# Bounded gathers with cleared row tiles in layer 2, adjacency pieces between x loads, and table 1 stored from GpSimd

## Chip, core and metric

The kernel runs on one core of one Trainium2 chip. The metric is the device time of one execution in microseconds (us). Lines such as L804 are lines of the kernel before. The engines are TensorE (PE in the profile), VectorE (DVE), ScalarE (ACT), GpSimd (POOL) and SyncE (SP).

## What is computed

Two graph attention layers on a graph of N = 2048 nodes, for a batch of 8, with 64 features, and a residual with two layer norms:

```python
mask = adj + eye(N) > 0
def _gat_layer(h, mask, b):            # h: [..., N, D]
    scores = einsum('...nd,...md->...nm', h, h)
    attn = softmax(where(mask, scores, NEG), axis=-1)
    return einsum('...nm,...md->...nd', attn, h) + b
h    = einsum('bnc,hdc->bhnd', x, Wh)              # 4 heads
z    = leaky_relu(concat_heads(_gat_layer(h, mask, bh)), 0.2)
h2   = einsum('bnk,dk->bnd', z, Wo)
z2   = leaky_relu(_gat_layer(h2, mask, bo), 0.2)
out  = layernorm(x + layernorm(z2) * gamma + beta)
```

The adjacency is sparse: the chance of a link is 0.0039 on the mean and falls with the square roots of both node numbers, so the first nodes have far more neighbours than the others.

## The kernel before

**Tiling.** The first 32 nodes (the hub) are computed against all nodes. The other 2016 are cut into 168 *sets* of 12 nodes. For each set the kernel finds the at most 128 nodes that any of its members is linked to, as a list of 128 node numbers, and gathers their rows. A row holds one node for all 8 batches: 4 pairs of 1 + 64 + 64 + 1 numbers (the ones give the softmax sums), 520 float32, 2080 bytes. Table 1 holds x, table 2 holds h2. Where a set has fewer than 128 neighbours, the places left over are *unlinked*: their index is N or more, and a mask takes them out of the sums later.

**Hub phase** (0 to 131 us). Loop L966 runs over 16 blocks of 128 nodes. In each step: load_x (L462) clears the ends of a row tile on VectorE and issues two DMAs of x from ScalarE; save_x (L469) stores the row tile, 260 KB, into table 1, from ScalarE; hub_scores (L597) multiplies, subtracts a mask on VectorE (L605) and takes the exp on ScalarE (L607); turn_x (L592) transposes the next block; hub_values (L611) sums. Meanwhile 34 *pieces* of the adjacency are loaded and prepared by load_adj (L674): the DMAs from SyncE, 440 KB a piece, into one of three raw tiles, then a conversion (L687) and diagonal marks (L695, L698) on GpSimd. more(n) (L943) takes the next n pieces. Before the loop stand more(6) (L949) and more(4) (L955), in it more(1) from i = 6 on (L969) and more(2) at i = 2 (L991). make_keys (L720) turns pieces into lists on TensorE, pick (L735) chooses the neighbours of 60 sets on VectorE.

**Layer 1** (131.7 to about 620 us). Loop L1133 runs over 84 groups of two sets: gather (L801, the instruction is L804) fetches the rows of table 1 on GpSimd, five groups ahead; then transposes, scores, mask (L839), exp, values and projections; the rows of table 2 are stored from SyncE (L910). Jobs for layer 2 are spread over it by ahead_of_second (L1125), one for each second group: among them memsets of shared tiles (L1126) and link() (L1066). In the last steps and after the loop (L1220) hub_step (L1118) computes the hub of layer 2 by parts: scores on TensorE (L1092), the mask's subtraction on VectorE (hub_lift2, L1101), exp on ScalarE (L1104), values.

**Layer 2** (627 to 904 us). There are 36 row tiles rowt2, and the 168 gathers use them in turn (rows2, L1235). The first 36 are issued ahead (L1242), the others nine steps ahead in loop L1425, which handles four sets per step u: turn2 (L1392) transposes the rows, scores2 (L1246) multiplies, exp, keep_scores (L1267) applies the mask *linked*, values2 (L1275) sums, and norm (L1289) does the layer norms, mostly on VectorE, in jobs spread over later steps.

**Bounds.** A gather may be given bounds_check = N - 1 with oob_is_err=False: places with a larger index are left out, and the tile keeps what it held. All gathers of layer 1 have it, and those of layer 2 from the 37th on. The first 36 of layer 2 haven't, as their tiles hold whatever lay in that memory; link() masks their indices to 0 to N - 1 instead, so that they fetch all 128 rows:

```python
bound = {} if layer == 2 and s < 36 else dict(bounds_check=N - 1, oob_is_err=False)
...
nc.vector.tensor_scalar(index2[:, :36], index2[:, :36], N - 1, None, OP.bitwise_and)
```

**What sets the order.** The schedule is manual: each engine runs its instructions in the order in which the program writes them, and engines wait for each other by semaphores, which the framework derives from the tiles read and written. DMAs are issued by the engine named (nc.sync, nc.scalar, nc.gpsimd), in the place where they stand in its program, and an issue waits like any other instruction.

Of the kernel before, what the change touches and what calls it, by code (L numbers as in the profile page):

```python
# [36 lines left out]
OP = mybir.AluOpType  # L37
# [322 lines left out]
def fast_kernel(ctx: ExitStack, tc: tile.TileContext, x, adj, Wh, bh, Wo, bo, gamma, beta, out, flag):  # L360


    nc = tc.nc
    B, N, C = x.shape
    H, D, _ = Wh.shape
    P = 128
# [61 lines left out]
    table1 = dram.tile([N, ROW], F32, name="table1")  # L428
# [9 lines left out]
    index = const.tile([P, NS], I32, name="index")  # L438
    index2 = const.tile([P, NS], I32, name="index2")
# [11 lines left out]
    xrow = {}  # L451
# [10 lines left out]
    def load_x(i):  # L462
        t = xrow[i] = rows_tile(f"x{i}")
        nc.vector.memset(t[:, :, 0:PW:PW - 1], 1.0)
        for p in range(2):
            nc.scalar.dma_start(out=t[:, :, 1 + p * D:1 + (p + 1) * D],
                                in_=x[p::2, i * P:(i + 1) * P, :].rearrange("q n c -> n q c"))

    def save_x(i):  # L469
        nc.scalar.dma_start(out=table1[i * P:(i + 1) * P, :], in_=xrow[i].rearrange("n q c -> n (q c)"))  # L470

    NCH = HALFN
    in_round = [min(FIRST, NS - FIRST * r) for r in range(NR)]
# [77 lines left out]
    def hub_mask():  # L551
        for k in range(2):
            nc.vector.tensor_scalar(hubm[:, k * NCH:(k + 1) * NCH], hubraw[k], 1.0, 0.0, OP.min, OP.max)
        nc.vector.tensor_tensor(hubm[:, :HUB], hubm[:, :HUB], identb[:HUB, :HUB], OP.max)
        pm = two("pm")
        for m in range(NB):
            nc.tensor.matmul(pm[:, m // 8, (m % 8) * HUB:(m % 8 + 1) * HUB], hubm[:, m * P:(m + 1) * P],
                             identb[:HUB, :HUB], start=True, stop=True)
        for k in range(2):
            nc.vector.tensor_scalar(  # L560
                maskh[:, k * 8:(k + 1) * 8, :].rearrange("p m (n h) -> p (m n) h", h=H),
                pm[:, k, :8 * HUB].unsqueeze(2).to_broadcast([P, 8 * HUB, H]), 0.0, 255.0, OP.is_equal, OP.mult)
        nc.vector.tensor_scalar(maskt[:HUB, NHB, :], pm[:HUB, 0, :HUB], 0.0, 255.0, OP.is_equal, OP.mult)
# [22 lines left out]
    def hub_columns():  # L586
        py = two("pyh")
        for h in range(H):
            nc.tensor.matmul(py[:, 0, h * P:(h + 1) * P], gram[:, h, :], xT[:, :, :HUB], start=True, stop=True)
        nc.vector.tensor_copy(yh.rearrange("p (m h) -> p m h", h=H), py[:, 0, :].rearrange("p (h m) -> p m h", h=H))  # L590

    def turn_x(i):  # L592
        tp = two(f"px{i}")
        turn(tp[:, 0, :], xrow[i])
        nc.scalar.copy(xT[:, :, i * P:(i + 1) * P], tp[:, 0, :].rearrange("c (q n) -> c q n", q=Q))

    def hub_scores(i):  # L597
        sp = two(f"sh{i}")
        for q in range(Q):
            for p in range(2):  # L600
                for r in range(2):
                    nc.tensor.matmul(sp[half(r), p, q * HW:(q + 1) * HW], xT[half(p), q, i * P + r * 64:i * P + (r + 1) * 64],
                                     yh[half(p), q * HW:(q + 1) * HW], start=True, stop=True)
        e = es[i % 2]
        nc.vector.tensor_tensor(e.rearrange("p (a q n) -> p a q n", a=2, q=Q), sp.rearrange("p a (q n) -> p a q n", q=Q),  # L605
                                maskh[:, i, :].unsqueeze(1).unsqueeze(1).to_broadcast([P, 2, Q, HW]), OP.subtract)
        nc.scalar.activation(e, e, AF.Exp, bias=shifts[:, 0:1], scale=1.0)  # L607
# [3 lines left out]
    def hub_values(i):  # L611

        for q in range(Q):
            for p in range(2):
                for u in range(2):
                    c0 = (p * Q + q) * HW + u * 64
                    o0 = q % 2 * PO + p * K1
                    nc.tensor.matmul(hubo[half(u), q // 2, o0:o0 + K1], es[i % 2][:, c0:c0 + 64], xrow[i][:, q, sums(p)],
                                     start=(i == 0 and q % 2 == 0 and p == 0), stop=(i == NB - 1), skip_group_check=True)
# [54 lines left out]
    def load_adj(r, t, m):  # L674

        s0 = FIRST * r + S10 * t
        ns = min(S10, NS - s0)
        np_ = ns * SET
        raw = early.tile([120, NCH], I32, tag="raw", name=f"raw{r}_{t}_{m}", bufs=3)
        for s, n0, n in flipped(s0, ns):  # L680
            nc.sync.dma_start(out=raw[s - s0:s - s0 + n], in_=adj[n0:n0 + n, m * NCH:(m + 1) * NCH])
        nc.sync.dma_start(out=raw[ns:np_], in_=byset[1:, s0:s0 + ns, m * NCH:(m + 1) * NCH])
        if m == 0:
            ahead[r, t] = early.tile([120, 2, HALFN + 80], BF16, tag="a", name=f"a{r}_{t}", bufs=5)
        a = ahead[r, t]
        w = NCH // 2
        nc.gpsimd.tensor_scalar(a[:np_, :, m * w:(m + 1) * w], raw[:np_].rearrange("p (c h) -> p h c", h=2),  # L687
                                1.0, 0.0, OP.min, OP.max)
        if m == 1:

            c1 = (REST + s0) // 2
            for h in range(2):
                for s, n0, n in flipped(s0, ns):
                    d = a[:np_, h, n0 // 2:(n0 + n) // 2]
                    nc.gpsimd.affine_select(out=d, in_=d, pattern=[[-2, n // 2]], base=s0 - s - h,  # L695
                                            channel_multiplier=1, compare_op=OP.not_equal, fill=1.0)
                d = a[:np_, h, c1:c1 + NS // 2 * (SET - 1)].rearrange("p (k c) -> p k c", k=SET - 1)[:, :, :ns // 2]
                nc.gpsimd.affine_select(out=d, in_=d, pattern=[[-ns, SET - 1], [-2, ns // 2]], base=-h - ns,  # L698
                                        channel_multiplier=1, compare_op=OP.not_equal, fill=1.0)
# [9 lines left out]
    def make_powers6():  # L709
        g = in_round[NR - 1] // S10 % 3  # L710
        d = powers6[:last * SET, g, 10 * g:10 * g + last]
        for k in range(SET):
            nc.gpsimd.affine_select(out=d, in_=d, pattern=[[-1, last]], base=-last * k, channel_multiplier=1,
                                    compare_op=OP.not_equal, fill=float(1 << k))
# [85 lines left out]

    def gather(table, s, layer, new):  # L801
        t = rows[layer, s] = new(f"g{layer}_{s}")
        bound = {} if layer == 2 and s < 36 else dict(bounds_check=N - 1, oob_is_err=False)
        nc.gpsimd.indirect_dma_start(out=t.rearrange("n q c -> n (q c)"), out_offset=None, in_=table,  # L804
                                     in_offset=bass.IndirectOffsetOnAxis(ap=(index if layer == 1 else index2)[:, s:s + 1], axis=0), **bound)

    def own_rows(m):

# [134 lines left out]
    def more(n):  # L943

        for _ in range(n):
            if pieces:
                load_adj(*pieces.pop(0))

    more(6)  # L949
    hub_mask()  # L950
    hub_mask_sets()
    weights()
    turn_x(0)
    hub_columns()
    more(4)  # L955
    picks = []

    def some(n):
        for _ in range(n):
            if picks:  # L960
                picks.pop(0)()
# [4 lines left out]
    for i in range(NB):  # L966
        if i + 4 < NB:
            load_x(i + 4)
        more(1 if i >= 6 else 0)  # L969
        save_x(i)  # L970
        if i == 3:
            nc.gpsimd.memset(rall[:, NG:, :], 1.0)
            nc.gpsimd.memset(rall2, 1.0)
            nc.gpsimd.memset(over, 0.0)
            for k in range(SET):
                nc.gpsimd.memset(bits[:, k:k + 1], N << k)
            nc.gpsimd.memset(shifts[:, 2:3], EPS)
            nc.gpsimd.memset(ones, 1.0)
            for t in rowts + xbs:
                nc.gpsimd.memset(t, 1.0)  # L980
            if last:
                make_powers6()
        hub_scores(i)
        if i + 1 < NB:
            turn_x(i + 1)
        if i:
            hub_values(i - 1)
        if i in (2, 6):
            make_keys(0, i // 6, two)
            if i == 2:  # L990
                more(2)  # L991
            if i == 6:
                picks = pick(0)
        some(4)
# [70 lines left out]
        nc.vector.tensor_tensor(index2, index2, node, OP.add)  # L1065

    def link():
        nc.vector.tensor_scalar(index2[:, :36], index2[:, :36], N - 1, None, OP.bitwise_and)
        nc.vector.tensor_scalar(linked, mask.rearrange("p s (k h) -> p s k h", h=H)[:, :, :, 0], 0.0, None, OP.is_equal)

    W2 = D + 2
# [161 lines left out]
    rowt2 = [late.tile([P, Q, PW], F32, name=f"rows2_{k}", bufs=1) for k in range(36)]  # L1233
# [7 lines left out]
        hub_block(8 + k, hrows[k])  # L1241
    for u in range(9):  # L1242
        for s in sets[u]:
            gather(table2, s, 2, rows2)

    def scores2(u):  # L1246
# [255 lines left out]
```

## Time and profile before

| what | us |
|---|---|
| median of 5 runs | 902.87 (901.93 to 907.39) |
| the profiled execution | 905.84 |
| its span, first to last instruction | 904.0 |
| busy: PE, DVE, ACT, POOL | 740.8, 602.8, 504.3, 516.2 |
| L804, gathers of layer 1 (168) | 178.5 busy, 1.062 each |
| L804, gathers of layer 2 (168) | 179.9 busy, 1.071 each |
| first and last gather of layer 2 start | 627.27, 856.60 |
| bytes of queue 0 (the gathers and other GpSimd DMAs) | 69.27 MB |

The span's mean granted TensorE clock is 0.942. The profile's timelines list, for each engine, start, length, line, operation, output and input tiles, and in square brackets the idle time ahead of the instruction and what ended it. "issue" means that nothing in the profile was waited for. The page's slices show TensorE busy over eight tenths from about 160 us on, with a dip in the slices at 610 to 650, where the profile shows both the lowest granted clock of the later part and the most DMA traffic (297 GB/s).

### The profile page before, as it was taken

The page shows a single profiled execution, that of the slowest core. Times are in us where ns is not written, and L with a number is a line of the kernel's source. Part 1 is how long each engine was busy: PE and PEld are TensorE (multiplying, and loading weights), DVE is VectorE, ACT ScalarE, POOL GpSimd, SP SyncE. Part 2 cuts the span into 40 slices and gives each one's busy share as a digit, 9 for nine tenths or more (in the row PEclk, how much of TensorE's full clock was granted, in tenths as well). Part 3 has the DMA queues.
Part 4 walks back from the last instruction along what each step waited for, and adds up shares of the span by engine and source line. Part 5 has one row for each costly group of instructions (what it writes and reads, how often), then busy time and mean ns, then how long its engine had stood idle before and what let it go on. Part 6 is the DMA issues. An engine that isn't in the chain of part 4 may idle for free. (4 is left out here: it accounts for less than half of the span.)

```text
span 904.0 us, 42354 instructions
## 1 busy us (share of the span) xinstructions
PE 740.8 (82%) x18079; PEld 654.1 (72%) x18079; DVE 602.8 (67%) x1380; ACT 504.3 (56%) x1038; POOL 516.2 (57%) x718
## 2 busy tenths in 40 slices
PE   2366647899999999999988999988998888878850
PEld 2345536788889889879878888877787788867640
DVE  3136962788978778775665565553238999888884
ACT  2022213567657666666654666663466777777731
POOL 5245227485445456556545667512777777777722
PEclk9988977999999999999988999997899999999975
DMA  7488825343333334444433444432985666666611
GB/s 118 131 229 224 226 65 152 86 143 101 81 82 89 94 93 132 126 118 136 120 107 110 127 126 135 115 93 71 297 269 161 189 191 185 187 188 190 191 46 37
DMA packets 82208, 125.69 MB, mean 139 GB/s; under 512 B 35318, under 2 KB 51374, under 8 KB 82012
## 3 DMA queue, kind: packets, MB, share of 16 engines
q0 software_dynamic: 27424, 69.27, 28.2%
q1 hardware_dynamic: 34888, 44.85, 16.6%
q10 hardware_dynamic: 19700, 8.78, 4.3%
q8 instruction: 145, 2.38, 1.1%
q14 instruction: 51, 0.42, 0.2%
HBM read 124.98 MB, written 18.48 MB: 159 GB/s over the span
## 5 line engine op out<-in xcount | busy, mean ns | idle before, releaser
L804 POOL DMA_INDIRECT g<-table,index x168 | 178.5, 1062 | 178.9 <-PE o L859 149.3
L804 POOL DMA_INDIRECT rows<-table,index x168 | 179.9, 1071 | 55.8 <-issue 25.3
L839 DVE TENSOR_TENSOR e<-s,mask 128x768 f32<-128x768 f32 x84 | 80.2, 955 | 81.3 <-PE s L834 78.3
L859 PE MATMUL o<-g,e 128*64 128x65 f32 x2688 | 101.5, 228 | 6.4 <-issue 6.4
L531 ACT ACTIVATE z<-cat,bhp 128x192 f32<-128x192 f32 x168 | 61.6, 418 | 79.6 <-PE cat L544 79.6
L525 PE MATMUL bank<-ident,g 128*128 128x128 f32 x672 | 102.6, 277 | 0.7 <-DVE keysi L773 0.7
L859 PEld LDWEIGHTS o<-g,e 128*64 128x64 f32 x2688 | 88.4, 140 | 18.4 <-issue 8.8
L834 PE MATMUL s<-y,xTg 64*64 64x48 f32 x5376 | 96.9, 220 | 1.2 <-DVE share L718 1.2
L1398 ACT COPY xts<-t 128x1024 f32<-128x1024 f32 x84 | 81.7, 1011 | 29.0 <-PE t L525 28.1
L834 PEld LDWEIGHTS s<-y,xTg 64*64 64x64 f32 x5376 | 86.6, 134 | 15.3 <-issue 15.2
L525 PE MATMUL t<-ident,rows 128*128 128x128 f32 x672 | 85.7, 277 | 10.7 <-DMA rows<-table,index 10.0
L1152 ACT COPY xTg<-bank 128x512 f32<-128x512 f32 x168 | 90.4, 597 | 1.0 <-PE bank L525 1.0
L825 ACT COPY y<-cat 128x384 f32<-128x384 f32 x80 | 41.0, 513 | 87.3 <-DVE rowt L907 51.5
L525 PEld LDWEIGHTS t<-ident,rows 128*128 128x128 f32 x672 | 75.8, 143 | 15.2 <-DMA rows<-table,index 9.5
L525 PEld LDWEIGHTS bank<-ident,g 128*128 128x128 f32 x672 | 82.4, 143 | 3.3 <-DVE keysi L773 1.2
L687 POOL TENSOR_SCALAR a<-raw 120x1024 bf16<-120x1024 int32 (+1 forms) x34 | 37.9, 1117 | 80.7 <-DMA raw<-in_adj_dram 45.5
L846 ACT ACTIVATE e<-e,shifts 128x768 f32<-128x768 f32 x84 | 81.0, 965 | 2.4 <-DVE e L839 2.1
L866 DVE RECIPROCAL rall<-o 64x8 f32<-64x8 f32 x168 | 34.5, 205 | 60.8 <-PE o L859 59.3
L819 PE MATMUL cat<-xo,gram 128*128 128x192 f32 x320 | 67.5, 335 | 0.0
L867 DVE TENSOR_TENSOR osb<-o,rall 128x512 f32<-128x512 f32 x84 | 58.1, 691 | 2.9
L607 ACT ACTIVATE e<-e,shifts 128x1024 f32<-128x1024 f32 x16 | 18.4, 1148 | 74.1 <-DMA x<-in_x_dram 24.1
L544 PE MATMUL cat<-otb,whT 64*64 64x96 f32 x1344 | 46.3, 250 | 13.3 <-ACT otb L883 11.6
(203 smaller groups left out, 1489.5 us busy)
## 6 DMA issues: line engine op xcount, KB each, us to landing
raw<-in_adj_dram SPq DMA_DIRECT2D x32, 440.0 KB
table<-xb SPq DMA_DIRECT2D x22, 256.0 KB
xr_s<-table SPq DMA_DIRECT2D x21, 256.0 KB
table<-x ACTq DMA_DIRECT2D x16, 260.0 KB
x<-in_x_dram ACTq DMA_DIRECT2D x32, 128.0 KB
table<-rowt SPq DMA_DIRECT2D x166, 24.4 KB
xb<-in_x_dram SPq DMA_DIRECT2D x168, 22.0 KB
out_dram<-y_s SPq DMA_DIRECT2D x144, 22.0 KB
```

What stands on the lines that cost most here:

```text
L525: nc.tensor.transpose(tp[:, q * P:(q + 1) * P], rows[:, q, 1:1 + P], ident)
L531: nc.scalar.activation(z[:, hp], cat[:, :, hp * n:(hp + 1) * n], AF.Identity, bias=bhp[:, hp:hp + 1], scale=1.0)
L544: nc.tensor.matmul(cat[half(j), s, hp * n:(hp + 1) * n], whT[half(s), h * D:(h + 1) * D], ot[half(s), h, :], start=True, stop=True)
L804: nc.gpsimd.indirect_dma_start(out=t.rearrange("n q c -> n (q c)"), out_offset=None, in_=table, in_offset=bass.IndirectOffsetOnAxis(ap=(in ...
L819: nc.tensor.matmul(cat[:, k, 2 * GM:2 * GM + n], gram[:, g % 2 * 2 + k, :], held["x", g // 2][:, :n], start=True, stop=True)
L834: nc.tensor.matmul(sp[half(r), p, (q * 2 + j) * M:(q * 2 + j + 1) * M], xt[half(p), j, q, half(r)], y[half(p), (j * Q + q) * M:(j * Q + q ...
L839: nc.vector.tensor_tensor(e[:, :16 * M].rearrange("p (a q n) -> p a q n", a=2, q=Q), sp[:, :, :8 * M].rearrange("p a (q n) -> p a q n", q= ...
L846: nc.scalar.activation(e[:, :16 * M], e[:, :16 * M], AF.Exp, bias=shifts[:, 0:1], scale=1.0)
L859: nc.tensor.matmul(op[half(p), j, o0:o0 + K1], e[:, c0:c0 + 64], rw[j][:, q, sums(p)], start=True, stop=True)
L867: nc.vector.tensor_tensor(osb, v[:, :, :, 1:K1], r.unsqueeze(3).to_broadcast([P, 4, 2, D]), OP.mult)
L1152: nc.scalar.copy(t[:, k, :], bank[k])
L1398: nc.scalar.copy(t, tp)
```

## The change

Three edits:

- **Layer 2.** All 168 gathers have bounds. Ahead of each of the first 36, in loop L1242, VectorE clears the gather's row tile, 128 x 520 float32, so that places left out hold zeros. The masking of the first 36 index columns in link() is removed.
- **Pieces.** more(6) ahead of the loop becomes more(4); the more(4) after hub_columns() and the more(2) at i = 2 are removed; loop L966 takes two pieces in each of steps 0 to 3, none in 4 and 5, one from 6 on. The order of the 34 pieces is the same; twelve of them are taken up to the same point of the program, i = 3 instead of i = 2.
- **Table 1.** save_x issues its store from GpSimd instead of ScalarE.

```diff
     def save_x(i):
-        nc.scalar.dma_start(out=table1[i * P:(i + 1) * P, :], in_=xrow[i].rearrange("n q c -> n (q c)"))
+        nc.gpsimd.dma_start(out=table1[i * P:(i + 1) * P, :], in_=xrow[i].rearrange("n q c -> n (q c)"))
...
     def gather(table, s, layer, new):
         t = rows[layer, s] = new(f"g{layer}_{s}")
-        bound = {} if layer == 2 and s < 36 else dict(bounds_check=N - 1, oob_is_err=False)
         nc.gpsimd.indirect_dma_start(out=t.rearrange("n q c -> n (q c)"), out_offset=None, in_=table,
-                                     in_offset=bass.IndirectOffsetOnAxis(ap=(index if layer == 1 else index2)[:, s:s + 1], axis=0), **bound)
+                                     in_offset=bass.IndirectOffsetOnAxis(ap=(index if layer == 1 else index2)[:, s:s + 1], axis=0),
+                                     bounds_check=N - 1, oob_is_err=False)
...
-    more(6)
+    more(4)
     hub_mask()
     hub_mask_sets()
     weights()
     turn_x(0)
     hub_columns()
-    more(4)
...
     for i in range(NB):
         if i + 4 < NB:
             load_x(i + 4)
-        more(1 if i >= 6 else 0)
+        more(2 if i < 4 else 1 if i >= 6 else 0)
         save_x(i)
...
             make_keys(0, i // 6, two)
-            if i == 2:
-                more(2)
...
     def link():
-        nc.vector.tensor_scalar(index2[:, :36], index2[:, :36], N - 1, None, OP.bitwise_and)
         nc.vector.tensor_scalar(linked, mask.rearrange("p s (k h) -> p s k h", h=H)[:, :, :, 0], 0.0, None, OP.is_equal)
...
     for u in range(9):
         for s in sets[u]:
+            nc.vector.memset(rowt2[s].rearrange("n q c -> n (q c)"), 0.0)
             gather(table2, s, 2, rows2)
```

## The prediction

> **What bounds the kernel now.** I began at the end, in the chain of waits that ended last. It runs back from the last output store through a chain of VectorE operations to a gather, and ahead of that lies nothing but gathers:
>
> ```profile
> 855.30 1.00 POOL rows L804
> 856.30 0.30 issue
> 856.60 4.44 DMA rows<-table,index
> 861.09 0.66 PE t L525 x4
> ```
>
> Columns are start, length, what. The last gather of layer 2 starts at 856.60, its rows land 4.44 later, TensorE turns them, and a tail of VectorE work ends the kernel. So the end is set by when the last of the 168 gathers runs. GpSimd's timeline shows how it gets there:
>
> ```profile
> 627.27 0.99 POOL L804 DMA_INDIRECT rows<-table,index  x1 [4.90 <-ACT share L1104]
> 628.57 0.96 POOL L804 DMA_INDIRECT rows<-table,index  x1 [0.30 <-issue]
> ...
> 672.42 1.01 POOL L804 DMA_INDIRECT rows<-table,index  x1 [0.30 <-issue]
> 673.74 1.01 POOL L804 DMA_INDIRECT rows<-table,index  x1 [0.30 <-PE t L525]
> ```
>
> Gather 0 starts at 627.27, 4.90 after GpSimd's last work (it needs the last rows of table 2 in memory, stored at 622 to 624); from there to 856.60 every idle gap is 0.30, the issue of the next gather. GpSimd is thus **never free** for 230 us: whatever delays gather 0, or lengthens any gather, moves the end by as much. TensorE doesn't hold the gathers back (no gap over 0.30 has its name).
>
> **Part 1: bounds on 36 more gathers.** The 36 gathers without bounds start at 627.27 to 671.17, a spacing of 43.90 / 35 = 1.254. The next ones, with bounds, are spaced 1.31 to 1.32 (672.42, 673.74) and 1.30 at the end (855.30, 856.60). So a bound costs about 0.052 of GpSimd time, and leaving places out doesn't shorten a gather. 36 x 0.052 = **+1.9**. What it saves is traffic: queue 0 carries 69.27 MB in the page; 36 full gathers are 36 x 266 KB = 9.6 MB, which leaves some 59.7 MB for 300 bounded ones, 199 KB each, so the change takes about 36 x 67 KB = 2.4 MB off. Is that worth time? The windows of gathers without and with bounds, and of the start:
>
> ```profile
> 627.20:672.40 45.20, 43.12 (x736) 37.70 (x736) 11.41 (x27) 22.11 (x33) 34.17 (x36) 0.86 0.92 277
> 620.00:640.00 20.00, 19.43 (x183) 16.93 (x183) 4.30 (x12) 4.22 (x9) 10.22 (x13) 0.57 0.54 141
> 640.00:660.00 20.00, 18.18 (x340) 15.44 (x339) 4.81 (x13) 12.06 (x17) 15.12 (x17) 1.00 1.03 315
> ```
>
> (stretch, length, busy time of PE, PEld, DVE, ACT, POOL, granted clock, DMA share, GB/s). The DMA engines are full here (1.03), yet the gathers go out at their own spacing all the same, so fewer bytes give nothing at the end. I count them 0. The removed masking of 36 indices in link() is one small VectorE operation in layer 1: 0.
>
> **Part 2: 36 memsets on VectorE.** In program order they stand behind hub_step(3) to (8), whose subtraction (L1101) runs on VectorE too:
>
> ```profile
> 633.50 0.42 DVE L1101 TENSOR_TENSOR share<-bank,maskt 120x256 f32<-120x256 f32 x1 [2.02 <-PE bank L1092]
> 635.94 0.42 DVE L1101 TENSOR_TENSOR share<-bank,maskt 120x256 f32<-120x256 f32 x1 [2.02 <-PE bank L1092]
> 640.76 0.42 DVE L1101 TENSOR_TENSOR share<-sh,maskt 120x256 f32<-120x256 f32 x1 [4.39 <-PE sh L1092]
> ```
>
> The sixth, hub_step(8), ends at 636.36, paced by TensorE at a granted clock of 0.57. VectorE works in order, so **memset 0 can't start before 636.36**, though VectorE is idle four fifths of 620 to 640. Gather 0, which now waits for memset 0, moves from 627.27 to 636.8: **+9.5** at the least. Queued behind the memsets are hub_step(9)'s subtraction (640.76) and the checks after it.
>
> A memset of 128x520: the rows of L1126 are 0.485 for 512 elements and 0.912 for 1024, a slope of 0.834 ns per element, so 0.434 for 520 where the fixed part overlaps, as it does between neighbours here (505.52 to 505.92 below). 36 x 0.434 = 15.6. The ends: by the spacing 0.40 of that row 14.7; by displacement (in the loop L867 to L536 is 0.60, with a memset between them 504.77 to 505.92, 1.15: +0.55 for 512) 36 x 0.558 = 20.1. I take 15.6, as memsets that follow one another depend on nothing.
>
> **Part 3: do the memsets block GpSimd?** This decides. Where a memset runs beside a gather in layer 1, the gather is long. VectorE, then GpSimd:
>
> ```profile
> 505.52 0.48 DVE L1126 MEMSET share<- 128x512 f32 x1
> 505.92 0.49 DVE L536 SCALAR_TENSOR_TENSOR z<-z 128x384 f32<-128x384 f32 x1
> ...
> 536.44 0.91 DVE L1126 MEMSET share<- 128x1024 f32 x1 [0.16 <-PE cat L819]
> 537.27 0.49 DVE L536 SCALAR_TENSOR_TENSOR z<-z 128x384 f32<-128x384 f32 x1
> ```
>
> ```profile
> 505.78 1.51 POOL L804 DMA_INDIRECT g<-table,index  x1 [0.30 <-issue]
> ...
> 536.60 2.04 POOL L804 DMA_INDIRECT g<-table,index  x1 [0.30 <-PE cat L819]
> ```
>
> The gather begun at 505.78 ends at 507.29, 0.88 after L536 ends (506.41); that of 536.60 ends at 538.64, 0.88 after L536 ends (537.76). Against 1.04 normally: +0.47 and +1.00, the difference about the longer memset. L536 alone doesn't explain it: a gather that had been running 0.34 when a two-input operation began beside it (733.31, operation at 733.65) took 1.00. So the memset held the gather, and then an operation that follows **without a gap** held it on. VectorE's 36 memsets would follow each other without a gap. By that, gather 0, let go by memset 0 at 636.8, gets nothing done until the train ends at 636.36 + 15.6 = 652.0, and ends at 652.8.
>
> [...]
>
> Sum of parts 1 to 3: gather 0 ends at 652.8 instead of 628.26, +24.5; the other 35 cost +1.8; the later 132 are as before. **+26.3.** Nothing catches up: GpSimd has no gap to give back. Consumers shift along: TensorE first turned rows at 636.36, and will when gathers 0 to 3 have landed (some 661), the same 9 after the stream's start as before, so the slots are freed in step.
>
> **Part 4: the hub phase** (stores of table 1 on GpSimd's queue, six adjacency pieces later). ScalarE:
>
> ```profile
> 36.06 4.00 ACTq L466 DMA_DIRECT2D x<-in_x_dram  x2
> 40.34 0.35 ACTq L470 DMA_DIRECT2D table<-x  x1
> 40.81 1.15 ACT L607 ACTIVATE e<-e,shifts 128x1024 f32<-128x1024 f32 x1 [16.66 <-DMA x<-in_x_dram]
> ```
>
> The first exp stands 16.66 behind x loads and a save that wait in ScalarE's queue. The saves go elsewhere, and x loads meet fewer adjacency pieces. What can come of it: make_keys(0,1) starts at 74.71 on TensorE, and it also needs adjacency converted on GpSimd at 64.95 to 66.97, so at most 74.7 - 67.0 = 7.7 is there to gain, and after it VectorE's picks set the pace up to 124.5 in any case. But the pieces between x loads are the same 34 in the same order: an x load that no longer stands behind pieces 5 to 10 stands behind two per step, and pieces that come later than 67 push make_keys back. Bounds: -5 (most of the 7.7) to +3 (a piece and its conversion late). I take **-1.4**, the four saves ahead of the fourth exp at 0.35 each. On GpSimd the 16 stores at 0.55 to 1.0 (its nearest DMA rows) are under 16 us and lie in its idle time, 23.98 ahead of 128.19; if that cover were gone, the first gather of layer 1 (131.66) would slip by what is left over.
>
> [...]
>
> **Total:** 26.3 - 1.4 = +24.9. The profiled execution took 905.84 (span 904.0), so it would take 930.7; the median shown, 902.87, lies 2.97 below it, so the forecast for a median is 902.87 + 24.9 = **927.8**. With the train at 20.1 it is 932.3, and with part 4 at its ends 924.2 to 932.2 for the 15.6.
>
> **Rivals.**
> - *B, half blocked.* GpSimd gets in between two memsets, as it does between dependent operations (the gather of 730.19 took 1.36, not two operations' length). Then gather 0 starts at 636.8 (+9.5), and in the 15.6 of the train some nine gathers are each about 0.45 longer, +4: 9.5 + 4 + 1.9 - 1.4 = +14.0, 916.9. For it: a memset signals a gather after each. Against it: 2.04.
> - *C, not blocked.* Only the late start counts: 9.5 + 1.9 - 1.4 = +10.0, 912.9. Against it the same rows.
> - *D, not slower.* No blocking, and part 4 pays in full: x loads and ScalarE, freed of pieces and saves, bring the first exp to about 33 from 40.81, make_keys to 67.0, and 7.7 goes through to layer 2. 9.5 + 1.9 - 7.7 = +3.7, 906.6, +0.4%. It holds from a hub gain of 6.9 on. Against it: the picks' pace after 79 and the pieces that make_keys needs.
> - *The change doesn't do what it says:* leaving places out saves 2.4 MB and no GpSimd time. That is in all cases.
>
> **Chances.** Forecast 0.60, B 0.18, C 0.15, D 0.04, slower still (train over 20, a hub phase that loses) 0.03. A measurement of this kernel tells about 0.5% (4.5 us) from no change. Slower 0.95, same 0.04 (D), faster 0.01. The likeliest case alone spans 923 to 936; the range goes down to C and up to the 20.1 train with a small loss in part 4: 911 to 935.
>
> **What would show it.** Right: the first layer-2 gather starting near 637 and lasting some 15; MEMSET rows from 636.4, spaced 0.41 to 0.56; L1101's seventh run near 652; the second gather near 653; bounded gathers from the start at 1.00 + 0.30; the last gather near 881; DMA GB/s at 640 to 652 near nothing. Wrong: a first gather of 1.0 (C), 1.4 to 1.8 (B); memsets that start before 636 (the late start falls); a first exp near 33 with make_keys at 67 (part 4 larger).

## The result and the profile after

The change is neither a loss nor much of a gain: median **900.63 us** (42 runs) beside 903.96 for the kernel before (79 runs), ratio 0.9963, 95% interval 0.9949 to 0.9978. The forecast was 927.8. The profiled execution took 900.75 (span 899.0).

GpSimd's timeline of the changed kernel, first and last gathers of layer 2 (line L803 now):

```profile
622.00 1.01 POOL L803 DMA_INDIRECT rows<-table,index  x1 [14.18 <-DMA hrows<-table]
623.32 1.00 POOL L803 DMA_INDIRECT rows<-table,index  x1 [0.31 <-issue]
624.63 1.00 POOL L803 DMA_INDIRECT rows<-table,index  x1 [0.30 <-DVE rows L1240]
...
850.76 1.00 POOL L803 DMA_INDIRECT rows<-table,index  x1 [0.31 <-issue]
852.06 1.26 POOL L803 DMA_INDIRECT rows<-table,index  x1 [0.30 <-PE t L525]
```

The gathers still go back to back, but the first starts at 622.00, 5.27 *earlier* than before, and it lasts 1.01. (Its label names a DMA, but in the program it waits for memset 0 and the stores of table 2, not for that DMA; it starts 1.24 to 1.25 after memset 0 does, here and in e1, e5, e10, e14 and e18.) VectorE beside them:

```profile
620.28 0.42 DVE L1097 TENSOR_TENSOR share<-bank,maskt 120x256 f32<-120x256 f32 x1 [2.02 <-PE bank L1088]
620.76 19.70 DVE L1240 MEMSET rows<- 128x520 f32 x36
640.38 0.69 DVE L1097 TENSOR_TENSOR share<-sh,maskt 120x256 f32<-120x256 f32 x2
```

The memsets stand where the prediction put them, behind hub_step(8) and ahead of hub_step(9), and take 19.70 in all. But 15 gathers of 0.99 to 1.01 run beside them: **the train holds nobody**. And hub_step(8) ends at 620.70 instead of 636.36. Where that comes from is seen at the other end of the kernel, on ScalarE:

```profile
25.01 3.95 ACTq L466 DMA_DIRECT2D x<-in_x_dram  x2
29.21 1.15 ACT L607 ACTIVATE e<-e,shifts 128x1024 f32<-128x1024 f32 x1 [6.36 <-DMA x<-in_x_dram]
```

The first exp is at 29.21 instead of 40.81, and the first gather of layer 1 at 120.81 instead of 131.66. The windows of the start of layer 2 (columns as in the prediction):

```profile
622.00:668.90 46.90, 35.88 (x630) 31.43 (x631) 24.97 (x55) 19.75 (x28) 35.93 (x36) 0.76 0.66 191
620.00:640.00 20.00, 9.09 (x65) 7.09 (x64) 17.67 (x37) 2.53 (x3) 13.98 (x14) 0.50 0.62 173
640.00:660.00 20.00, 18.66 (x332) 16.74 (x336) 5.41 (x14) 11.92 (x18) 15.18 (x16) 0.88 0.75 227
```

The DMA engines are no longer full (0.75 where it was 1.03), and the gathers are no faster for it: 36 of them take 46.91 where they took 45.15.

The two profiles, step by step (the store is the last that ScalarE issues, and the time is the end of its issue):

| | before | after | difference |
|---|---|---|---|
| first gather of layer 1 | 131.66 | 120.81 | -10.85 |
| last store of table 2 issued | 624.30 | 609.75 | -14.55 |
| gather 0 of layer 2 | 627.27 | 622.00 | -5.27 |
| gather 36 | 672.42 | 668.91 | -3.51 |
| gather 167 | 856.60 | 852.06 | -4.54 |
| span | 904.0 | 899.0 | -5.0 |

Read as a sum: hub phase -10.85, layer 1 -3.70, the wait for memset 0 +9.28, bounds +1.76, the other gathers -1.03, the tail -0.46. The -3.70 belongs to these two profiles: from the first gather to the last store of table 2 it is 492.6 in before and 488.9 here, but 493.4 and 491.2 in two later runs (e14, e15) with the same hub edits.

The chain that ended last no longer runs through the last gather. At the end it goes over output stores on SyncE and loads of the residual:

```profile
849.65 0.66 SPq L1363
850.35 0.41 SPq L1363
851.20 2.69 DMA xr_s<-table
```

The two ways are near each other: from the last gather to the end of the span it is 46.9, before 47.4.

### The profile page after: what moved, and what is told of

Same layout as the page of the kernel before. It is cut to its first block, busy times and chain, and to the rows that moved or that the text cites. A ratio compares the mean times of both kernels' runs of the same rounds, so it can differ in the third digit from the quotient of the medians.

```text
span 899.0 us, 42480 instructions
## 1 busy us (share of the span) xinstructions
PE 739.2 (82%) x18079; PEld 652.8 (73%) x18079; DVE 619.1 (69%) x1415; ACT 502.8 (56%) x1038; POOL 523.8 (58%) x734
## 3 DMA queue, kind: packets, MB, share of 16 engines
q0 software_dynamic: 28704, 71.12, 29.2%
## 4 chain that ended last, share of the span: by engine, by line
PE 50%; DVE 18%; DMA 12%; issue 8%; SPq 5%; ACT 3%; POOL 2%; ACTq 0%; POOLq 0%; DVEq 0%
PE o L859 11%; PE s L834 9%; PE bank L525 7%; PE cat L819 5%; SPq L1363 5%; DMA raw<-in_adj_dram 5%; PE cat L544 4%; PE o L876 3%; PE cat L893 3%; DMA out_dram<-y_s 3%; DMA x<-in_x_dram 2%; PE cat L903 2%; DVE rows L1240 2%; DVE st_s L1314 2%; DVE y_s L1334 2%
## 5 line engine op out<-in xcount | busy, mean ns | idle before, releaser
L803 POOL DMA_INDIRECT g<-table,index x168 | 178.3, 1062 | 176.4 <-PE o L859 146.9
L803 POOL DMA_INDIRECT rows<-table,index x168 | 180.4, 1074 | 65.1 <-issue 15.2
L834 PEld LDWEIGHTS s<-y,xTg 64*64 64x64 f32 x5376 | 86.4, 134 | 15.4 <-issue 15.2
L525 PE MATMUL t<-ident,rows 128*128 128x128 f32 x672 | 87.2, 280 | 11.7 <-DMA rows<-table,index 11.5
L819 PE MATMUL cat<-xo,gram 128*128 128x192 f32 x320 | 65.7, 328 | 0.0
L867 DVE TENSOR_TENSOR osb<-o,rall 128x512 f32<-128x512 f32 x84 | 58.0, 691 | 2.9
```

The lines of the kernel that those rows point to most:

```text
L525: nc.tensor.transpose(tp[:, q * P:(q + 1) * P], rows[:, q, 1:1 + P], ident)
L819: nc.tensor.matmul(cat[:, k, 2 * GM:2 * GM + n], gram[:, g % 2 * 2 + k, :], held["x", g // 2][:, :n], start=True, stop=True)
L834: nc.tensor.matmul(sp[half(r), p, (q * 2 + j) * M:(q * 2 + j + 1) * M], xt[half(p), j, q, half(r)], y[half(p), (j * Q + q) * M:(j * Q + q ...
L867: nc.vector.tensor_tensor(osb, v[:, :, :, 1:K1], r.unsqueeze(3).to_broadcast([P, 4, 2, D]), OP.mult)
```

## The experiments

**How to read the ratios.** Beside e13 to e15 the kernel before took 902; beside e1 to e12 and e16 to e18 it took 1034 to 1037, and one chip showed both. Only the first is the condition of the result. Most of what differs is layer 2: from its gather 0 to the end of the span it is 276.7 in the profile of before and 386.3 in e3, beside which before took 1034. The hub phase is the same (131.7 and 131.6), and from there to gather 0 of layer 2 it is 495.6 and 511.7. The waits from 700 to 850 us, of e3 and then of before:

```profile
POOL rows L804 <- PE o L1283: 63.9, 21, 26.6
...
PEld bank L1253 <- issue: 21.9, 28, 3.0
```

```profile
PEld bank L1253 <- issue: 2.9, 17, 0.2
```

Columns are the total, how often, the longest. In e3 GpSimd waits 63.9 for TensorE, and TensorE's weight loads have 21.9 of idle time in front of them that nothing in the profile explains. In before it is 2.9, and no wait of GpSimd is over 0.31. So where before takes 1035, gathers aren't the limit of layer 2, and a late gather 0 is hidden. Why it does is not settled. The hub phase and the start of layer 2 can be read from either.

### The two halves by themselves

e1, e5, e10 and e18 are one kernel, the layer-2 part; e2, e6, e11 and e15 another, the hub part. As edits of the changed kernel and of the one before:

```diff
# e1, e5, e10, e18: the change with the hub part undone
-        nc.gpsimd.dma_start(out=table1[...
+        nc.scalar.dma_start(out=table1[...
-    more(4)
+    more(6)
...
+    more(4)
-        more(2 if i < 4 else 1 if i >= 6 else 0)
+        more(1 if i >= 6 else 0)
+            if i == 2:
+                more(2)
# e2, e6, e11, e15: the kernel before with just these lines as in the change
```

> Only the layer-2 part of the change (bounds and memsets on the first 36 gathers, masking removed); hub phase as before. Theory T (two effects of opposite sign: the hub phase is 11 to 14 us shorter, the layer-2 part costs its late start of 9.3 us and 36 x 0.052 us for the bounds, and memsets don't hold gathers): +11 us, about 915 where before is 904; first layer-2 gather at about 637, each 1.00 long. Rival R (the recorded prediction: a train of memsets holds GpSimd): +26, about 930, first gather lasting over 10 us. Rival S (the change's layer-2 part costs nothing, since the sum came out near zero): 904.

> Only the hub part (adjacency pieces between x loads, table 1 stored from GpSimd); layer 2 as before. Theory T: first layer-1 gather at about 121 instead of 131.7, table 2 complete 11 to 14 us earlier, the first layer-2 gather right after it, total 890 to 893. Rival S: the hub phase's gain is lost in layer 1, total near 900. Recorded prediction: -1.4, 902.5.

> The kernel of e1_layer2 again, as the chip of e1 to e4 ran the kernel before at 1033.66 with gathers of layer 2 that wait for TensorE, not back to back. Where before is near 904 and the gathers go back to back, theory T: +9.3 (late start) + 1.9 (bounds) = +11, ratio 1.012. Recorded prediction: +26, ratio 1.029. Rival S (the part is free on any chip): ratio 1.000.

> The kernel of e2_hub again. Theory T on a chip where before is near 904: first layer-1 gather near 121, first layer-2 gather near 613 to 616, total 890 to 893 (ratio 0.985 to 0.988). Rival: the hub gain is lost in layer 1 and the ratio is that of the whole change, 0.996.

> The kernel of e1 (layer-2 part only) once more. On a chip where before takes about 904, theory T: ratio 1.012 (+11), recorded prediction 1.029, rival S 1.000. On one where before takes about 1035, as e1 and e5: 0.998 to 1.001, since gathers wait for TensorE there.

> The kernel of e2 (hub part only) once more. On a chip where before takes about 904, theory T: ratio 0.985 to 0.988 (890 to 893); rival (gain lost in layer 1): 0.996. Where before takes about 1035, as e2 and e6: 0.990 to 0.992.

Measured, all where before takes 1034 to 1037: layer-2 part 1.0003 (0.9972 to 1.0034), 0.9987 (0.9957 to 1.0017), 1.0025 (0.9994 to 1.0056); hub part 0.992 (0.9889 to 0.995), 0.990 (0.9866 to 0.9933), 0.9918 (0.9884 to 0.9952). First gather of layer 1: 135.55, 136.11, 135.24 with the layer-2 part, 121.31, 122.88, 124.16 with the hub part. So the hub part carries a gain to the end, and rival S holds for layer 2 under this condition. To settle it under the other condition, the two parts were run again:

> The whole change, on the chip of this call. If before takes about 904: ratio 0.996, as recorded with the result. If about 1035: the hub part (0.991) and the layer-2 part (0.999 to 1.002) add up to 0.990 to 0.993; first layer-2 gather 9 us after table 2 is complete either way.

> The hub part alone, beside e14. Where before takes about 904: ratio 0.985 to 0.988, faster than the whole change by 9 to 11 us, which would be the cost of the layer-2 part. Where about 1035: 0.990 to 0.992, equal to e14 within 3 us.

> The layer-2 part alone (kernel of e1). Where before takes about 904, theory T: first gather 6 to 9 us later than before's 627, total +6 to +10, ratio 1.007 to 1.011; recorded prediction 1.029; rival S 1.000.

e14 (the whole change): 899.53, ratio 0.9945 (0.9901 to 0.999), before 902.42. e15 (hub part): **893.56**, ratio 0.9896 (0.9836 to 0.9955). GpSimd in e15 and in e14:

```profile
614.04 0.99 POOL L804 DMA_INDIRECT rows<-table,index  x1 [4.90 <-DVE share L1098]
...
843.12 1.19 POOL L804 DMA_INDIRECT rows<-table,index  x1 [0.30 <-PE t L525]
```

```profile
623.65 1.01 POOL L803 DMA_INDIRECT rows<-table,index  x1 [10.74 <-DMA hrows<-table]
...
853.36 1.00 POOL L803 DMA_INDIRECT rows<-table,index  x1 [0.30 <-PE t L525]
```

In e15 gather 0 starts 2.98 after the last store of table 2 is issued (611.06), in e14 8.83 after (614.82). Between the medians lies 899.53 - 893.56 = +6.0 for the layer-2 part; 9 to 11 were expected, and the ratios' intervals overlap, so this size is loose. The wait isn't: 8.83, 8.82, 8.83, 8.83 and 8.83 in e1, e5, e10, e14 and e18, 2.89 to 3.01 wherever gather 0 waits for no memset. That is +5.9. In the profile after it was 12.25, +9.3, as hub_step(5) to (8) were 2.45 apart there and 1.64 in e14: VectorE reaches the memsets later. TensorE, which paces these steps, had a granted clock of 0.54 there (609.7 to 620.7); from hub_step(3) to (4), still at 1.00 (608.70 to 610.26), it took 1.56, beside 1.57 in e14. Between the profiles of e15 and e14 (spans 891.4 and 901.0) the 9.6 are 5.85 for the wait, 1.86 for gathers 0 to 36, 3.76 ahead of the wait, where the two kernels have the same edits but for the small masking in link(), and -1.87 behind gather 36. e18 fell where before takes 1034 again: 0.9991 (0.9964 to 1.0018), so the layer-2 part by itself was not measured where before takes 904.

### Saves or pieces

```diff
# e3: the kernel before with
-        nc.scalar.dma_start(out=table1[...
+        nc.gpsimd.dma_start(out=table1[...
# e4: the kernel before with the pieces of the change, saves on ScalarE
# e13: the kernel before with
     hub_columns()
+    load_x(4)
+    load_x(5)
     more(4)
...
-        if i + 4 < NB:
+        if 2 <= i and i + 4 < NB:
             load_x(i + 4)
# e16: the kernel before with
-    more(6)
+    more(4)
...
     hub_columns()
-    more(4)
+    more(6)
```

> Only the 16 stores of table 1 moved from ScalarE's queue to GpSimd's. If the saves held ScalarE (rival H1): first exp near 36, first layer-1 gather 5 us or more earlier, total 897 to 899. If the pieces ahead of the x loads held it (theory H2): first exp still near 40.8, gain under 2 us, total 902 to 904.

> Only the adjacency pieces moved between the x loads; saves stay on ScalarE. H2 (the pieces ahead of the x loads hold the first exp): first exp near 30, first layer-1 gather 8 to 11 us earlier, total 891 to 896. H1 (the saves do): gain under 3 us, total 901 to 904. If both are needed: each alone under half of the gain of both.

> The kernel before, with the x loads of blocks 4 and 5 issued ahead of the four adjacency pieces 7 to 10 instead of in steps 0 and 1 of the loop; nothing else moved. Theory P (an x load waits for the landing of a DMA some places ahead of it in the program, so ten pieces ahead of it hold it, and ScalarE behind it): first exp near 30 instead of 41, the first layer-1 gather 3 to 8 us earlier, ratio 0.993 to 0.997. Rival W (the x loads wait for DMA bandwidth that the pieces take): first exp still near 41, ratio 1.000.

> The kernel before with four adjacency pieces first and six after hub_columns() instead of six and four; all ten still stand ahead of the loop, saves on ScalarE. In the built program the x loads of block 4 then wait for the landing of the third piece, as with the whole change, instead of the fifth. Theory P2 (what piece an x load waits for decides): first exp at 29 to 32 instead of 41, first layer-1 gather 4 to 9 us earlier, ratio 0.991 to 0.996. Rival Q (the pieces must stand between the x loads of the loop): first exp near 41, ratio 1.000.

e3: 0.9994 (0.9961 to 1.0026), first exp 40.83, first gather 131.56: the saves by themselves bring nothing. e4: 0.9884 (0.9845 to 0.9923), first exp 30.79, first gather 123.35: it is the pieces. e13: 1.0011 (0.998 to 1.0043), first exp *later*, first gather the same. ScalarE, then GpSimd, in e13:

```profile
36.85 7.44 ACTq L466 DMA_DIRECT2D x<-in_x_dram  x4
48.19 0.35 ACTq L470 DMA_DIRECT2D table<-x  x1
48.65 1.15 ACT L607 ACTIVATE e<-e,shifts 128x1024 f32<-128x1024 f32 x1 [26.44 <-DMA x<-in_x_dram]
```

```profile
131.62 1.12 POOL L804 DMA_INDIRECT g<-table,index  x1 [0.47 <-DVE rall L625]
```

The loads were called earlier in the program and issued no earlier. The built program says why: each DMA issued by SyncE or ScalarE takes the next of eight completion semaphores and waits until that one's last DMA has landed, and the x loads of block 4 wait for the landing of the *fifth* piece, in before and in e13 alike. In the trace of before the last part of that piece lands at 39.66 and the second of the two loads is issued at 39.69; in that of after it is the third piece, and the times are 28.57 and 28.59. e13 put two more loads ahead of the exp, and the save ahead of it now waits for the seventh piece, in before for the sixth: hence the later exp. It does not speak for rival W, since it didn't change what the loads of block 4 wait for. e16 does: with four pieces first, block 4's loads wait for the *third* piece. ScalarE and GpSimd:

```profile
22.87 4.16 ACTq L466 DMA_DIRECT2D x<-in_x_dram  x2
29.86 0.35 ACTq L470 DMA_DIRECT2D table<-x  x1
30.32 1.15 ACT L607 ACTIVATE e<-e,shifts 128x1024 f32<-128x1024 f32 x1 [8.11 <-DMA x<-in_x_dram]
```

```profile
120.11 1.12 POOL L804 DMA_INDIRECT g<-table,index  x1 [0.39 <-DVE rall L625]
```

Ratio 0.9907 (0.9871 to 0.9943): these two numbers, 6 and 4 to 4 and 6, give as much as the hub part (0.990 to 0.992), with saves on ScalarE and no piece in steps 0 and 1 of the loop. P2 holds, Q falls; W was not tried by itself. The waits of later loads and saves move along with that of block 4 (block 5's loads are issued from 33.69 on, in before from 47.73), and which waits between 23 and 62 us hand it on from the x loads to the adjacency was not tried.

### What holds a gather

```diff
# e8: the change with (flat2[s] is row tile s as 128 x 520), in loop L1238,
-            nc.vector.memset(rowt2[s]...
+            if s < 35:
+                nc.vector.memset(flat2[s + 1], 0.0)
+            if s < 12:
+                nc.vector.tensor_tensor(flat2[s], flat2[s], flat2[s], OP.add)
+            elif s < 24:
+                nc.vector.tensor_scalar(flat2[s], flat2[s], 1.0, None, OP.mult)
             gather(table2, s, 2, rows2)
# and the memset of flat2[0] ahead of the loop
# e9: the same, with in place of the addition and the multiplication
+                nc.vector.tensor_reduce(small[:, s:s + 1], flat2[s], AX.X, OP.add)
+                nc.vector.tensor_reduce(small[:, s:s + 1], flat2[s][:, :64], AX.X, OP.add)
```

> The whole change with one more VectorE instruction per tile behind the memset of the next tile: for tiles 0 to 11 a two-input addition of the tile to itself, for 12 to 23 a multiplication by 1 (one input), from 24 on memsets alone. Theory M (a memset holds no gather; a two-input operation does, also while it waits behind a memset): gathers beside the additions 1.5 to 2.0 long, ending about 0.87 after an addition ends; beside memsets alone 1.00. Rival G (a memset holds a gather unless a gap follows it): gathers beside the multiplications are long as well, since they follow the memsets without a gap. Rival N (neither holds): all 1.00.

> The whole change, with a sum over the tile (tensor_reduce, one input) in place of the addition or multiplication of e8 behind each memset: 520 elements for tiles 0 to 11, 64 for 12 to 23, memsets alone from 24 on. It too follows the memset without a gap. Theory M (only certain operations hold a gather: two inputs, or the fast copy-like form that took 0.36 in e8; a memset or a sum doesn't): all gathers 1.00. Rival G (a memset holds a gather whenever the next operation follows without a gap): gathers beside the sums 1.5 to 2.0.

VectorE and GpSimd in e8:

```profile
652.84 0.49 DVE L1243 MEMSET rows<- 128x520 f32 x1
653.25 0.64 DVE L1245 TENSOR_TENSOR rows<-rows 128x520 f32<-128x520 f32 x1
...
661.65 0.49 DVE L1243 MEMSET rows<- 128x520 f32 x1
662.06 0.36 DVE L1247 TENSOR_SCALAR rows<-rows 128x520 f32<-128x520 f32 x1
```

```profile
652.86 1.89 POOL L803 DMA_INDIRECT rows<-table,index  x1 [0.30 <-DVE rows L1245]
...
661.67 1.62 POOL L803 DMA_INDIRECT rows<-table,index  x1 [0.30 <-DVE rows L1247]
...
673.22 1.00 POOL L803 DMA_INDIRECT rows<-table,index  x1 [0.30 <-DVE rows L1243]
```

The gather of 652.86 ends at 654.75, 0.86 after the addition ends (653.89); that of 661.67 ends at 663.29, 0.87 after the multiplication (662.42). Beside memsets alone a gather takes 1.00. So behind a memset both operations hold a gather, the one-input multiplication too. M as worded here doesn't settle it: a memset followed without a gap could still be the cause (G). e9 decides, with a sum that follows without a gap, again VectorE and GpSimd:

```profile
648.60 0.49 DVE L1244 MEMSET rows<- 128x520 f32 x1
649.01 0.63 DVE L1246 TENSOR_REDUCE small<-rows 128x1 f32<-128x520 f32 x1
```

```profile
645.99 1.01 POOL L803 DMA_INDIRECT rows<-table,index  x1 [11.84 <-DMA hrows<-table]
647.30 1.00 POOL L803 DMA_INDIRECT rows<-table,index  x1 [0.30 <-issue]
648.61 1.00 POOL L803 DMA_INDIRECT rows<-table,index  x1 [0.30 <-DVE small L1246]
```

The gather of 648.61 stands to its memset and sum as that of 652.86 to its memset and addition. All gathers of e9 beside memsets and sums take 0.99 to 1.01, so G falls: without the addition or multiplication behind it, a memset holds nothing. But the memset matters too, as rows of the profile before show. VectorE, then GpSimd:

```profile
311.79 0.69 DVE L867 TENSOR_TENSOR osb<-o,rall 128x512 f32<-128x512 f32 x1
312.40 0.55 DVE L536 SCALAR_TENSOR_TENSOR z<-z 128x384 f32<-128x384 f32 x1
```

```profile
312.34 1.01 POOL L804 DMA_INDIRECT g<-table,index  x1 [0.30 <-issue]
```

Here L536 (the leaky ReLU, two inputs) follows L867 without a gap and begins 0.06 after the gather, and the gather is not held. In the 20 profiles of this case an L536 begins 0.03 to 0.75 after the start of a gather 180 times. In the 100 where it stands behind a memset the gather ends 0.86 to 0.88 after L536. In 72 where it stands behind L867, a copy or another two-input operation, the gather takes 1.00 to 1.07; in the other 8 a one-input operation of 1.20 holds it, and L536 behind that adds nothing. So it takes the pair, a memset and L536 behind it, for L536 to hold a gather that began before it. For the addition and the multiplication of e8 no row has them without the memset. Nor is a memset the only such neighbour: the gather of 683.17 in before took 1.73 and ended 0.87 after L1313, a two-input operation begun 0.18 after it behind another one, L1322, that was running when it began. Why the neighbour in front matters is not shown. (e8 took 1031.2 and e9 1026.5, one run each, where before took 1037.)

### The first twelve gathers as before

```diff
# e7, e12, e17: the whole change, with
+        bound = {} if layer == 2 and s < 12 else dict(bounds_check=N - 1, oob_is_err=False)
...
+        nc.vector.tensor_scalar(index2[:, :12], index2[:, :12], N - 1, None, OP.bitwise_and)
...
-            nc.vector.memset(rowt2[s]...
+            if s >= 12:
+                nc.vector.memset(rowt2[s]...
```

> The whole change, but gathers 0 to 11 of layer 2 without bounds, memset and wait, as before; 12 to 35 with. Theory T: gather 0 starts when table 2 is complete, 9 us earlier than with the change; gather 12 comes 15 us later, when its memset is done; total the change minus 9 to 10, near 891, within 2 us of e6. If the late start costs nothing (rival S): total as the change, 900.

> The kernel of e7 (the whole change with gathers 0 to 11 as before) once more. On a chip where before takes about 904, theory T: the change minus 9, ratio 0.986 (891); rival S (the late start costs nothing): 0.996. Where before takes about 1035, as e7: 0.982.

> The whole change with gathers 0 to 11 of layer 2 as before (kernel of e7). Where before takes about 904, theory T: first layer-2 gather 3 us after table 2 is complete, near 614, total 891 to 894, ratio 0.988 to 0.990, equal to the hub part alone. Rival S (the late start costs nothing): as the whole change, 0.995.

0.9816 (0.9776 to 0.9856), 0.9873 (0.9846 to 0.9901), 0.9843 (0.981 to 0.9876), all where before takes 1034 to 1037; gather 0 starts 2.97 to 3.01 after the last store of table 2. The wait is gone, and the medians are the lowest there: 1019.24, 1022.0 and 1017.79, which is 8.1 and 5.8 under the hub part measured beside them (e6, e11) and 5.1 under e16. The intervals overlap for the last two, and theory T expected e7 within 2 us of e6. Why it comes out lower, where a late gather 0 costs nothing, is not shown. Where before takes 904 it was not run; there the fastest shown is e15.

## Why the prediction was wrong

**Part 3 failed: "the memset held the gather".** It rested on gathers of 1.51 and 2.04 beside L1126 in layer 1, and on ruling out L536, the operation that follows. Those gathers are as long in the changed kernel, 2.04 at 526.05 for one. That L536 alone doesn't explain them was right (1.01 at 312.34). But the memset alone doesn't either: beside the train and beside e9's memsets and sums a gather takes 0.99 to 1.01. What holds it is the pair, a memset with L536 behind it, as with the addition and the multiplication of e8; behind a memset of the train stands only the next memset. So the step from "memset and L536" to "memset after memset" failed, and with it go 15.2 of the 26.3: the wait from 636.8 to 652.0.

**Part 4 was mis-sized: -1.4 (bounds -5 to +3) for what measured -10.85** at the first gather of layer 1 (-10.2 and -11.7 in e14 and e15; in all profiles with the hub edits it starts at 119.91 to 124.18), -8.9 in e15's median. The prediction capped the gain at 7.7 because the twelfth piece was converted and marked at 64.95 to 66.97. That time was not fixed: its conversion starts at 59.09 now, and make_keys(0,1) went from 74.71 to 61.95. And the wait in ScalarE's queue was read rightly in the 16.66 ahead of the first exp, but not followed to what the x loads waited for, a piece's landing. The -1.4 was put on the saves, which by themselves bring nothing (e3).

**The late start (+9.5) was right in kind.** +9.3 in the profile after, +5.9 in the five others, where the hub steps come closer together (1.64 apart in e14; in the profile after, the one pair at a granted clock of 1.00 is 1.56 apart). The prediction took its 9.5 from a profile with 2.45 between them, and named the clock of 0.57 there without asking what another clock would make of it. It is counted from table 2's end, so the hub's gain moves it along.

**Bounds (+1.9): right**, +1.76. **Fewer bytes: right**, 2.4 MB (queue 0 has 73.53 MB with the hub part, stores of table 1 included, and 71.12 with the whole change) and no time that shows where gathers go back to back. **Memset: mis-sized** and without effect: one is 0.492, spaced 0.549, so 19.70 and not 15.6; between two memsets there are 0.057 of gap, and the displacement, 20.1, was the better reading.

**The rivals.** D had both mechanisms, no blocking and a hub phase that pays in full; its price for the hub phase, 7.7, was too low, and so its time, 906.6, too high. C had the late start right, and erred in part 4. By the medians of e15 and e14 it is -8.9 for the hub part and +6.0 for adding layer 2's, -2.9 for the whole, beside -3.3 in the result. A change that seems to do little is a gain and a loss of nearly one size.

## What to carry to other kernels

Take a change of several edits apart before believing its sum: here reverting the layer-2 edits gives 893.56 where the whole gives 899.53. When an engine's queue waits for a load, follow it to what the *load's issue* waits for; a bound drawn from another time in the same profile holds only if nothing that the change moves feeds that time. When two operations stand back to back beside a long instruction, one such row can't say which of them holds it: look for rows that have each without the other, and test each with another neighbour.

## What the hardware showed that was not expected

- A two-input addition or a one-input multiplication on VectorE held a GpSimd gather that started before it, with a memset running ahead of it without a gap (gathers of 1.89 and 1.62 in e8). A memset followed by a sum or a memset doesn't (0.99 to 1.01), and L536 holds one behind a memset (1.51, 2.04) but not behind L867 (1.01).
- A gather takes 1.00 with bounds and 0.95 without (35.93 and 34.17 for 36), although the bounds save 2.4 MB over 36 gathers.
- The same program took 902 and 1034 to 1037 at different times, both on one chip. Most of the difference is in layer 2 (276.7 and 386.3), with TensorE's weight loads idle for up to 3.0 with nothing to wait for in the profile. The cause is open.
